# A Mamba and expert layer on one core: the bias as one bf16 matmul, one state's C taken from PSUM, scattering DMAs set to other steps

## The chip, the core and the metric

The kernel runs on one core of a Trainium2 chip. The core has five engines with an in-order queue each: TensorE (PE), VectorE (DVE), ScalarE (ACT), GpSimd (POOL) and SyncE (SP, which here only issues DMAs). The metric is the device time of one execution in microseconds. Three runs of the kernel before gave 952.07, 952.93 and 959.26 us; the median is 952.93.

## The reference, cut to what matters

The input x is 8 sequences of 512 tokens with 128 features. Two branches work on the normalized x: a Mamba layer that runs forward and backward over the sequence, and a router that sends each token to one of 8 experts. Both are added to x.

```python
def mamba(x, ...):                                # f: forward, b: on x[:, ::-1]
    xi, z = split(x @ in_w.T)                     # 256 channels each
    xi = silu(causal_conv(xi) + conv_b)
    dt, Bm, Cm = split(xi @ x_w.T, [8, 8 + 16])   # 16 states
    delta = softplus(dt @ dt_w.T + dt_b)
    h[t] = h[t-1] * exp(delta[t] * A) + delta[t] * u[t] * Bm[t]   # for each state
    y[t] = sum over states of h[t] * Cm[t]
    return ((y + xi * Dp) * silu(z)) @ out_w.T
out = concat([out_f, out_b]) @ combine_w.T + combine_b
...
e = argmax(xn @ router_w.T)                       # expert of each token
ffn = (silu(xn @ gate_w[e].T) * (xn @ up_w[e].T)) @ down_w[e].T
```

The change touches three places of it: the addition of `combine_b`, the product `h * C` of one state, and when the tokens are written out in the order of their experts.

## The kernel before, in words

**Units, states, steps.** A unit is one sequence in one direction; there are 16, f and b in turn (unit 0 is f, 1 is b, 2 is f and so on). A unit has 16 states, and one loop step does one state of one unit: step s is state s mod 16 of unit s div 16, 256 steps in all (L1113 to L1136). Channels lie on the partitions in two halves h, tokens along the free dimension.

**One state.** ACT makes `dA = exp(delta * A)` (L771). The term `b` is made in PSUM: either ACT scales the token-major `dut` by B (L787) and PE transposes it back (L800), or PE spreads B's row over the partitions by a bf16 matmul with a selecting weight (L805) and DVE multiplies by `du` (L812). DVE scans `h` over the tokens (L818, twice 128x512). POOL multiplies `hs` by C for both halves at once (`times_c`, L841, 128x1024). C's row, spread over 128 partitions, comes from DRAM as the tile `cs`: SP issues that DMA three steps ahead (L778), into one of 6 buffers. PE then adds the state into `py` by transposes (L855, `sum_up`, three steps later). In the last unit only, for states 11, 13 and 15, C is spread by a PE matmul into PSUM (`spread_c`, L830), no `cs` is loaded, and DVE does the product as two 128x512 instructions (L839). That choice is `c_in_psum`. The PSUM tile comes from the pool `ps_mm` (2 banks), which nearly everything else that PE makes uses too.

**Around the states.** A plan, written out by hand as (step, kind), calls other work between the states. `prepare(v)` makes unit v's inputs during unit v-1: at its step 9 `log1p` on POOL (L689, and L691 where DVE does not add the last term), at 9 also `split(1)`, at 11 and 12 `delta` on DVE (L698 and the following lines), which reads what `log1p` made (`w`) and what PE made (`pd`, L650). `conclude(v)` finishes unit v during unit v+1: the gate on DVE, two turns by PE, at step 7 and 8 `project` (L914, four token blocks in two halves, into the PSUM tile `po`), at step 9 `total`, where DVE adds `po` to `xt` (L929). In an f unit `project` ends each half with a float32 matmul of one row of ones with `combine_b` (L921, 1x256). In b units there is no bias.

**Scattering.** When the experts of all tokens are known, 32 indirect DMAs write the tokens in the order of the experts (`scatter`, L409). POOL issues them, one at the start of a step ("ev"), at step `35 + i*37//32`, so from 35 to 70 without the steps 42, 49, 57 and 64. Step 35 to 47 is unit 2, 48 to 63 is unit 3 (49 and 57 are free there), 64 to 70 unit 4. At step 73 SP loads the first group of sorted tokens (L434), which waits for all scatters. Within a step, what `prepare` put at "ev" stands ahead of the scatter, and both stand ahead of the step's product on POOL.

**Setup.** POOL fills the constants (L129 to L175), then weights (L185), then `selector` (L194); `split` follows when ACT has made `cdt` (L646). All weights come in one packed tensor `pk`; `combine_b` is its row 0.

Of the kernel before, what the change touches and what calls it, by code (L numbers as in the profile page):

```python
# [33 lines left out]
BF16 = mybir.dt.bfloat16  # L34
# [5 lines left out]
P = 128  # L40
EPS = 1e-5
DIRS = ("f", "b")
L, D, DI, R, NS, KC, E = 512, 128, 256, 8, 16, 4, 8
NH, NJ = DI // P, L // P
# [5 lines left out]
LAST_BY_ACT, LAST_C = BY_ACT + (4, 6, 10, 12, 14), (11, 13, 15)  # L50

ROWS, ROW_C, ROW_DT = 3 * NS, 64, 96
NX = ROW_DT + R


def columns():
# [20 lines left out]
def block_kernel(ctx: ExitStack, tc: tile.TileContext, a: dict, out: bass.AP):  # L77
    nc = tc.nc
    x = a["x"]
    NB = x.shape[0]  # L80
    NT = NB * NJ
# [8 lines left out]
    const, big, tmp = pool("const", 1), pool("big", 1), pool("tmp", 1)  # L90
    two, stp, rep, ffn = pool("two", 2), pool("stp", 4), pool("rep", 6), pool("ffn", 4)
# [12 lines left out]
    at, width = columns()  # L104
    pk = const.tile([P, width], F32, name="pk")
# [10 lines left out]

    rout = pk[:, at["rout"]]
    comb = halves("comb", D)
    comb_b = pk[0:1, at["comb_b"]]
    w = {}  # L120
    for i, d in enumerate(DIRS):
        w[d, "in"] = pk[:, at[d, "in"]]
# [29 lines left out]
    ones = const.tile([P, P], F32, name="ones")  # L152
# [35 lines left out]
    def selector():  # L188


        nothing = const.tile([P, 1], F32, name="nothing")
        nc.vector.memset(nothing, 0.0)
        for k in range(3):
            nc.gpsimd.affine_select(  # L194
                out=sel,
                in_=sel if k else nothing[:ROWS].unsqueeze(2).to_broadcast([ROWS, NS, P]), compare_op=ALU.not_equal, fill=1.0,
                base=-k * NS, pattern=[[-1, NS], [0, P]], channel_multiplier=1,
            )

    def project_weights(d, di):  # L200
        mo = const.tile([P, NH, D], F32, name=f"{d}_mo")
# [206 lines left out]
    def scatter(t):  # L408
        i = nc.gpsimd.indirect_dma_start(  # L409
            sorted_in[:, :], bass.IndirectOffsetOnAxis(ap=M["row"][:, t : t + 1], axis=0),  # L410
            xn[t // 8][:, t % 8, :], None,
        )

        tc.declare_no_dep(i.ins, group="scatter", reason="every token has a row of its own")
        tc.add_to_no_dep_group("scatter", i.ins)
# [106 lines left out]
    units = [(b, d) for b in range(NB) for d in DIRS]  # L522
# [236 lines left out]
        return s % NS in sets.get(s // NS, BY_ACT)  # L759

    def c_in_psum(s):
        return s >= NSTEP - NS and s % NS in LAST_C

    def decay(s):

# [107 lines left out]
    def conclude(v):  # L873
        b, d = units[v]
        c = C[v]

        def gate(ks=range(0, NJ, 2)):
            if "yt" not in c:
                c["yt"] = tmp.tile([P, NJ, DI], F32, tag="yt", name=f"yt_{v}")
            for k in ks:  # L880
                nc.vector.tensor_mul(
                    c["yt"][:, k : k + 2], c["py"][:, k : k + 2], c["z"][:, k : k + 2]
                )

        def turned(dst, j, h):
            if d == "f":
                nc.tensor.transpose(dst, c["yt"][:, j, h * P : (h + 1) * P], ident)
            else:
                nc.tensor.matmul(
                    dst, c["yt"][:, NJ - 1 - j, h * P : (h + 1) * P], exch,  # L890
                    start=True, stop=True,
                )

        def block(y, h, j):
            return y[:, h, j, :] if len(y.shape) == 4 else y[:, h, j * P : (j + 1) * P]

        def back(h):

            p = c["pyb", h] = mm([P, L], f"pyb_{v}{h}")
            for j in range(NJ):  # L900
                turned(p[:, j * P : (j + 1) * P], j, h)

        def back_end(h):
            if h == 0:
                c["y"] = tmp.tile([P, NH, L], F32, tag="y", name=f"y_{v}")
            nc.scalar.copy(c["y"][:, h, :], c["pyb", h])

        def project(js=range(NJ), whole=True):
            if whole or js[0] == 0:
                c["po"] = mm([P, NJ, D], f"po_{v}_{js[0]}")  # L910
            p = c["po"]
            for j in js:
                for h in range(NH):
                    nc.tensor.matmul(  # L914
                        p[:, j, :], block(c["y"], h, j), w[d, "mo"][:, h, :],
                        start=(h == 0 and (d == "b" or j == js[0])),
                        stop=(d == "b" and h == NH - 1), skip_group_check=(d == "f"),
                    )
            if d == "f":

                nc.tensor.matmul(  # L921
                    p[:, js[0] : js[-1] + 1, :], ones[0:1, :],
                    comb_b.unsqueeze(1).to_broadcast([1, len(js), D]),
                    start=False, stop=True, skip_group_check=True,
                )

        def total(js=range(NJ)):
            xs = xt[:, b * NJ + js[0] : b * NJ + js[-1] + 1, :]
            nc.vector.tensor_add(xs, c["po"][:, js[0] : js[-1] + 1], xs)  # L929

        def by_pairs():

            y = tmp.tile([P, NJ, NH, P], F32, tag="y", name=f"y_{v}")
            c["y"] = y.rearrange("p j h t -> p h j t")
            pairs = [range(k, k + 2) for k in range(0, NJ, 2)]
            for i, js in enumerate(pairs):
                gate((NJ - 2 - js[0],) if d == "b" else (js[0],))
                p = c["pyb", i] = mm([P, 2, NH, P], f"pyb_{v}{i}")
                for j in js:
                    for h in range(NH):  # L940
                        turned(p[:, j - js[0], h, :], j, h)
                copy = nc.scalar.copy if i == 0 else nc.vector.tensor_copy
                copy(y[:, js[0] : js[-1] + 1], p)
            for js in pairs:
                project(js)
                total(js)
                nc.sync.dma_start(
                    out[b].rearrange("(j p) h -> p j h", p=P)[:, js[0] : js[-1] + 1, :],
                    xt[:, b * NJ + js[0] : b * NJ + js[-1] + 1, :],
                )  # L950

        if v == len(units) - 1:
            return [(2, "dv", by_pairs)]
        do = lambda f, *k: lambda: f(*k)
        return [
            (2, "dv", gate),
            (3, "pe2", do(back, 0)), (4, "ev", do(back_end, 0)),
            (4, "pe2", do(back, 1)), (5, "ev", do(back_end, 1)),
            (7, "pe", do(project, range(2), False)),
            (8, "pe", do(project, range(2, NJ), False)), (9, "dv", total),  # L960
        ]

# [8 lines left out]
    def add(step, kind, f):  # L971
        plan[step, kind].append(f)
# [29 lines left out]
    for i, kind in (  # L1002
        (0, "dv"), (1, "ev"), (1, "dv"), (1, "pe2"), (2, "ev2"), (2, "dv"),
        (3, "dv"), (4, "ev"), (4, "dv"), (5, "ev"),
    ):
        add(o + i, kind, lambda: next(order_of, None))
    for i in range(NT):
        add(o + 6 + i * 37 // NT, "ev", lambda i=i: scatter(i))

    begin = 4  # L1010
    groups = [list(range(k, min(k + GROUP, NK))) for k in range(0, NK, GROUP)]
# [37 lines left out]
        pass  # L1049
    weights("f")  # L1050
    selector()
    first.norm()
    first.turn()
    first.turn_end()
# [155 lines left out]
```

## Time and profile before

| | busy us | share of the span | instructions |
|---|---|---|---|
| PE matmul | 850.2 | 89% | 5510 |
| PE weight load | 657.9 | 69% | 5510 |
| DVE | 907.2 | 95% | 1101 |
| ACT | 803.0 | 84% | 1490 |
| POOL | 841.5 | 88% | 524 |

The profiled execution has a span of 951.6 us and a time of its own of 953.34 us. The granted PE clock was 0.953 on average. Where the kernel's lines spend their time:

| line | what | count | busy us | mean ns |
|---|---|---|---|---|
| L841 | POOL product with C, 128x1024 | 253 | 594.3 | 2362 |
| L818 | DVE scan, 128x512 | 512 | 592.8 | 1206 |
| L839 | DVE product with C from PSUM, 128x512 | 6 | 3.8 | 679 |
| L830 | PE matmul that spreads C | 6 | 3.4 | 640 |
| L914 | PE projection, f units | 128 | 16.9 | 275 |
| L921 | PE bias, 1x256 float32 | 32 | 11.1 | 425 |
| L805 | PE spreading B, 48x512 bf16 | 125 | 50.6 | 405 |
| L409 | POOL issues a scatter | 32 | 32.5 | 1015 |
| L689 | POOL part of log1p, 128x1024 | 15 | 35.4 | 2361 |

A float32 matmul appears as two instructions, and matmuls overlap, so their means are longer than the time from one start to the next. "Idle before" of an instruction is how long its engine stood still ahead of it, with the engine and line that ended the wait.

### The profile page before, as it was taken

How to read it: one execution, taken by the hardware profiler on the slowest of the kernel's cores; microseconds unless marked ns; L12 is line 12 of the kernel's file. 1: busy time of each engine (PE TensorE's matmuls, PEld its weight loads, DVE VectorE, ACT ScalarE, POOL GpSimd, SP SyncE). 2: the span in 40 equal slices, each digit the busy share in tenths (PEclk: the TensorE clock that was granted, in tenths of full speed). 3: DMA queues.
4: the chain of work that ended last, by engine and by line, in shares of the span. 5: the costliest groups of instructions: out<-in, count | busy, mean ns of one | idle time of the engine just before them, and what ended most of it. 6: DMA issues, size and time to landing. Idle time of an engine off the chain costs nothing.

```text
span 951.6 us, 16224 instructions
## 1 busy us (share of the span) xinstructions
PE 850.2 (89%) x5510; PEld 657.9 (69%) x5510; DVE 907.2 (95%) x1101; ACT 803.0 (84%) x1490; POOL 841.5 (88%) x524
## 2 busy tenths in 40 slices
PE   5699896978789889899998999989999999989897
PEld 2367574766567668777786877868777786767676
DVE  7999989999899999999999999999999999999996
ACT  5898986969679797998969989698988979799792
POOL 5689798799999979799897998979899898979995
PEclk9588999988979999999899999999999999999999
DMA  5364222222233625245441544425245341622262
GB/s 153 111 132 107 66 76 66 78 74 80 84 95 104 192 70 182 78 123 163 114 154 53 161 138 121 152 82 185 63 130 168 112 153 54 186 74 85 90 177 75
DMA packets 68483, 108.54 MB, mean 114 GB/s; under 512 B 6848, under 2 KB 29248, under 8 KB 68400
## 3 DMA queue, kind: packets, MB, share of 16 engines
q1 hardware_dynamic: 65552, 101.32, 36.0%
q0 software_dynamic: 2272, 4.67, 1.4%
q10 hardware_dynamic: 576, 1.51, 0.5%
q8 instruction: 44, 0.72, 0.3%
q14 instruction: 39, 0.32, 0.1%
HBM read 97.60 MB, written 9.87 MB: 113 GB/s over the span
## 4 chain that ended last, share of the span: by engine, by line
PE 42%; ACT 26%; DVE 18%; issue 7%; POOL 6%; DMA 1%; SPq 0%; POOLq 0%; DVEq 0%; ACTq 0%
PE py L855 14%; DVE hs L818 10%; ACT dA L771 8%; PE b L800 7%; ACT dbt L787 7%; PE pg L457 4%; PE pd L650 4%; POOL hs L841 3%; DVE b L812 3%; DVE acc L590 2%; PE pde L489 2%; PE po L914 2%; PE b L805 2%; ACT acc L582 1%; PE pdu L714 1%
## 5 line engine op out<-in xcount | busy, mean ns | idle before, releaser
L841 POOL TENSOR_TENSOR hs<-hs,cs 128x1024 f32<-128x1024 f32 x253 | 594.3, 2362 | 71.9 <-DVE hs L818 59.9
L818 DVE TENSOR_TENSOR_SCAN hs<-dA,b 128x512 f32<-128x512 f32 x512 | 592.8, 1206 | 0.1
L855 PE MATMUL py<-ident,hs 128*128 128x128 f32 x2048 | 279.3, 282 | 10.8 <-POOL hs L841 10.7
L855 PEld LDWEIGHTS py<-ident,hs 128*128 128x128 f32 x2048 | 234.4, 145 | 47.2 <-POOL hs L841 23.6
L787 ACT ACTIVATE dbt<-dut,bt 128x256 f32<-128x256 f32 x524 | 221.9, 496 | 0.1
L800 PE MATMUL b<-ident,dbt 128*128 128x128 f32 x1048 | 187.5, 289 | 19.6 <-DVE hs L818 10.4
L771 ACT ACTIVATE dA<-delta,b_A 128x512 f32<-128x512 f32 x256 | 168.2, 715 | 14.9 <-DVE hs L818 14.8
L800 PEld LDWEIGHTS b<-ident,dbt 128*128 128x128 f32 x1048 | 128.8, 145 | 74.1 <-ACT dbt L787 52.7
L771 ACT ACTIVATE dA<-delta,f_A 128x512 f32<-128x512 f32 x256 | 168.6, 715 | 8.3 <-DVE hs L818 6.3
L812 DVE TENSOR_TENSOR b<-du,b 128x512 f32<-128x512 f32 x250 | 159.8, 686 | 9.3 <-PE b L805 8.5
L599 PE MATMUL pz<-pk,xin 128*128 128x256 f32 x128 | 42.8, 492 | 29.3 <-DVE acc L590 25.4
L650 PE MATMUL pd<-cdt,pk 9*128 9x512 f32 x124 | 66.3, 635 | 0.0
L590 DVE SCALAR_TENSOR_TENSOR acc<-pi,pk,acc 128x511 f32<-128x511 f32 (+2 forms) x96 | 64.5, 739 | 0.1
L457 PE MATMUL pg<-xeT,we 128*128 128x128 f32 x468 | 61.8, 278 | 2.2 <-ACT z L610 2.1
L457 PEld LDWEIGHTS pg<-xeT,we 128*128 128x128 f32 x468 | 56.2, 192 | 5.5 <-ACT z L610 3.8
L599 PEld LDWEIGHTS pz<-pk,xin 128*128 128x128 f32 x128 | 30.2, 247 | 41.1 <-ACT dbt L787 26.5
L805 PE MATMUL b<-cdt,sel 48*128 48x512 bf16 x125 | 50.6, 405 | 8.6 <-DVE hs L818 8.6
L721 ACT COPY dut<-pdu 128x512 f32<-128x512 f32 x32 | 18.6, 585 | 34.6 <-PE pdu L714 34.6
L500 POOL DMA_INDIRECT by_token<-ye,to x39 | 39.6, 1016 | 6.3 <-issue 3.1
L646 POOL TENSOR_TENSOR cdt<-cdt 32x512 f32<-32x512 f32 (+1 forms) x32 | 33.1, 1034 | 7.8 <-ACT cdt L632 7.7
L489 PEld LDWEIGHTS pde<-we,g 128*128 128x128 f32 x234 | 27.6, 191 | 15.2 <-issue 7.6
L409 POOL DMA_INDIRECT sorted_in<-xn,row_i x32 | 32.5, 1015 | 5.3 <-issue 3.8
(170 smaller groups left out, 1054.8 us busy)
## 6 DMA issues: line engine op xcount, KB each, us to landing
cs<-cd SPq DMA_DIRECT2D x253, 256.0 KB, 3.5
we<-in_expert_w SPq DMA_DIRECT2D x39, 576.0 KB, 4.6
sorted_in<-empty SPq DMA_DIRECT2D x9, 258.0 KB, 7.9
xe<-sorted_in SPq DMA_DIRECT2D x9, 258.0 KB, 4.5
xt<-in_x SPq DMA_DIRECT2D x8, 256.0 KB, 7.3
moe<-by_token SPq DMA_DIRECT2D x8, 256.0 KB, 3.0
out<-xt SPq DMA_DIRECT2D x7, 256.0 KB, 3.7
pk<-in_pack ACTq DMA_DIRECT2D x1, 704.0 KB, 7.9
```

Source lines behind the costliest of these rows:

```text
L457: nc.tensor.matmul(p[:, q - 4 * b, :], T[ks[i]][:, which, c, :], G[ks[0], "xT"][:, i, :], start=True, stop=True,)
L590: nc.vector.scalar_tensor_tensor(c["acc"][:, h, k:], c["pi", h][:, : L - k], cw[:, h, KC - 1 - k : KC - k], c["acc"][:, h, k:], ALU.mult, ...
L599: nc.tensor.matmul(p[:, j, :], c["xin"][:, t : t + P], w[d, "in"][:, DI:], start=True, stop=True,)
L650: nc.tensor.matmul(p, w[d, "dt"][:, h * P : (h + 1) * P], cdt[ROW_DT : NX + 1], start=True, stop=True,)
L771: nc.scalar.activation(k["dA"][:, h, :], c["delta"][:, h, :], AF.Exp, scale=w[d, "A"][:, h, n : n + 1],)
L787: nc.scalar.activation(k["dbt"][:, j, :], c["dut"][:, j, :], AF.Copy, scale=c["bt"][:, j, n : n + 1],)
L800: nc.tensor.transpose(k["b", h][:, j * P : (j + 1) * P], k["dbt"][:, j, h * P : (h + 1) * P], ident,)
L805: nc.tensor.matmul(k["b", 0], sel[:, n, :], c["bc"], start=True, stop=True)
L812: nc.vector.tensor_mul(k["b", h], c["du"][:, h, :], k["b", 0])
L818: nc.vector.tensor_tensor_scan(k["hs"][:, h, :], k["dA"][:, h, :], k["b", h], 0.0, ALU.mult, ALU.add)
L841: nc.gpsimd.tensor_mul(k["hs"], k["hs"], k["cs"].unsqueeze(1).to_broadcast([P, NH, L]))
L855: nc.tensor.matmul(c["py"][:, j, h * P : (h + 1) * P], block[:, h, j * P : (j + 1) * P], weight, skip_group_check=True, **kw,)
```

## The change

It has three parts. The bias: `combine_b` is packed three times, on rows 0 to 2; at the start POOL takes from rows 0 and 1 what bf16 keeps of them, and from row 0 once more, so that the upper halves of the three rows are three bf16 pieces of the float32 bias. `project` of an f unit then begins with one bf16 matmul of 3 rows and 512 columns over the whole of `po`, instead of ending each half with a float32 one. The product: in unit 3, state 6 (step 54), C goes the way of the last unit's states 11, 13, 15. The scatters: 32 steps from 35 to 71, without 40, 48, 52, 55 and 66.

```diff
+SCATTER, SCATTER_C = 3, (6,)
...
-    comb_b = pk[0:1, at["comb_b"]]
+    comb_b = pk[0:3, at["comb_b"]]
+    bias = comb_b.bitcast(BF16).rearrange("p (n two) -> p n two", two=2)[:, :, 1]
+    one_row = const.tile([3, P], BF16, name="one_row")
+    nc.gpsimd.memset(one_row, 1.0)
...
+    def bias_pieces():
+        for m in (2, 1):
+            nc.gpsimd.tensor_sub(comb_b[:m], comb_b[:m], bias[:m])
...
     def c_in_psum(s):
-        return s >= NSTEP - NS and s % NS in LAST_C
+        return s % NS in {SCATTER: SCATTER_C, len(units) - 1: LAST_C}.get(s // NS, ())
...
         def project(js=range(NJ), whole=True):
-            if whole or js[0] == 0:
+            new = whole or js[0] == 0
+            if new:
                 c["po"] = mm([P, NJ, D], f"po_{v}_{js[0]}")
             p = c["po"]
+            if new and d == "f":
+                nc.tensor.matmul(
+                    p, one_row, bias.unsqueeze(1).to_broadcast([3, NJ, D]),
+                    start=True, stop=False, skip_group_check=True,
+                )
             for j in js:
                 for h in range(NH):
                     nc.tensor.matmul(
                         p[:, j, :], block(c["y"], h, j), w[d, "mo"][:, h, :],
-                        start=(h == 0 and (d == "b" or j == js[0])),
-                        stop=(d == "b" and h == NH - 1), skip_group_check=(d == "f"),
+                        start=(d == "b" and h == 0), stop=(h == NH - 1),
+                        skip_group_check=(d == "f"),
                     )
-            if d == "f":
-                nc.tensor.matmul(
-                    p[:, js[0] : js[-1] + 1, :], ones[0:1, :],
-                    comb_b.unsqueeze(1).to_broadcast([1, len(js), D]),
-                    start=False, stop=True, skip_group_check=True,
-                )
...
+    dates = [s for s in range(o + 6, o + 6 + 37) if s not in (40, 48, 52, 55, 66)]
     for i in range(NT):
-        add(o + 6 + i * 37 // NT, "ev", lambda i=i: scatter(i))
+        add(dates[i], "ev", lambda i=i: scatter(i))
...
     selector()
+    bias_pieces()
...
-    pack[0, at["comb_b"]] = inputs[pre + "combine_b"]
+    pack[:3, at["comb_b"]] = inputs[pre + "combine_b"]
```

(`o` is 29 there, so that `o + 6` is step 35.)

## The prediction

> **What bounds the kernel.** First the busy table: DVE is busy 95% of the span, so its idle time is what can be won. DVE's timeline lists each idle stretch with what ended it. Between step 0 and the last 50 us these are mostly 0.2 to 1 us of waiting for PE, and two larger waits for POOL, with a third, small one behind them:
>
> ```profile
> 196.97 0.70 DVE L698 SCALAR_TENSOR_TENSOR pd<-pd,w 128x512 f32<-128x512 f32 x1 [1.85 <-POOL w L691]
> ...
> 257.56 0.70 DVE L698 SCALAR_TENSOR_TENSOR pd<-pd,w 128x512 f32<-128x512 f32 x1 [4.02 <-POOL w L689]
> ...
> 313.96 0.70 DVE L698 SCALAR_TENSOR_TENSOR pd<-pd,w 128x512 f32<-128x512 f32 x1 [0.18 <-POOL w L689]
> ```
>
> The bracket is DVE's idle time before `delta`. All three are where `delta` needs POOL's `log1p`, called at steps 41, 57 and 73, for units 3, 4 and 5. Next POOL's timeline there:
>
> ```profile
> 251.84 1.01 POOL L409 DMA_INDIRECT sorted_in<-xn,row_i  x1 [0.17 <-issue]
> 252.88 2.34 POOL L841 TENSOR_TENSOR hs<-hs,cs 128x1024 f32<-128x1024 f32 x1
> 255.18 2.35 POOL L689 TENSOR_TENSOR w<-q,w 128x1024 f32<-128x1024 f32 x1
> ...
> 306.90 4.71 POOL L841 TENSOR_TENSOR hs<-hs,cs 128x1024 f32<-128x1024 f32 x2
> 311.56 2.37 POOL L689 TENSOR_TENSOR w<-q,w 128x1024 f32<-128x1024 f32 x1
> ```
>
> From 170.97 to 329 us POOL's only idle time is the 0.17 before each scatter. A product with its scatter takes about 3.57 us there, about a DVE step. POOL is behind: at 252.88 it starts the product of step 56, while DVE has ended the scans of step 59 at 253.54. So from 171 to 314 `log1p` arrives when POOL's list is done, and the list sets the time. After 329 POOL waits again (5.35 us at 346 for a scan), and DVE leads, with PE close behind. The f units' bias is in PE's timeline, here of unit 9, where unit 8 is projected, with DVE beside it:
>
> ```profile
> 588.30 0.40 PE L805 MATMUL b<-cdt,sel 48*128 48x512 bf16 x1
> 588.63 1.09 PE L855 MATMUL py<-ident,hs 128*128 128x128 f32 x8
> ...
> 590.77 0.69 PE L921 MATMUL po<-pk,ones 1*128 1x256 f32 x2
> 591.39 1.16 PE L457 MATMUL pg<-xeT,we 128*128 128x128 f32 x8
> ```
> ```profile
> 592.59 0.69 DVE L481 TENSOR_TENSOR g<-g,pg 128x512 f32<-128x512 f32 x1 [0.38 <-PE pg L457]
> ...
> 602.64 0.69 DVE L698 SCALAR_TENSOR_TENSOR delta<-pd,w 128x512 f32<-128x512 f32 x1 [0.24 <-PE pd L650]
> ```
>
> PE runs without a gap there, and DVE twice waits for it behind the bias.
>
> **Scatters and the product.** A scatter costs POOL 1.01 + 0.17 = 1.18 us, wherever it stands; all 32 stay. A product costs 2.33 from start to start (4.66 for two: 2.36 + 2.30). Before step 41's `log1p` stand 6 scatters now and 5 then: the 1.85 wait falls by 1.18. Step 42 takes one instead, so POOL is level again. Before step 57's stand 20 now and 18 then, and the product of step 54 is gone: 2 x 1.18 + 2.33 = 4.69, so `w` ends at 257.53 - 4.69 = 252.84. DVE takes over that product as two instructions, 1.28 us a pair at the end of this kernel, 1.20 to the next start. It comes to `delta` at 253.54 - 1.18 - 0.35 (a wait for `po` at 247.20, below) + 1.20 = 253.2. So the 4.02 wait goes and 4.3 us are won there.
>
> Then it is partly handed back. Before step 73's `log1p` stand 32 scatters in both kernels, so POOL's list is shorter by the product alone: `w` ends at 313.93 - 2.33 = 311.60. DVE, which came at 313.78, comes at 309.5 and waits 2.1. What remains is 313.96 - 311.62 = **2.34 us**. POOL cannot run out of work meanwhile: its smallest lag behind DVE's scan in the stretch is 3.4 us (step 67, scan end 289.49, product 292.89), and there POOL is earlier by 2.33 + 1.18, one product and one scatter, and DVE by 4.3: the lag grows.
>
> Beside that, at no cost: PE's C matmul (1.05 us in the chain of the last unit) lies where PE waits for POOL (14 us of waits for POOL's products from 206 to 262); were that cover gone it would cost its 1.05. It takes one of the two banks of `ps_mm`, and PE's `pd` now stands behind DVE's product; `pd` began at 238.28, and the scan before the product ended at 236.29, so bank and PE are ready in time, and a delay up to 4 us would fall into the wait that goes. One `cs` DMA less. The last scatter goes from step 70 to 71, and SP's load of sorted tokens waits for it (3.4 us now); `cs` loads queue behind that. It is POOL's list that sets when it is issued: 303.54 now, about 303.4 then. The `cs` load issued behind it at 306.98 lands 3.5 later and is used at 321.82: 11 us of room. At the start POOL makes the pieces: two instructions smaller than the 1.03 of L646, within its 7.68 us of waiting before 22.08; the memset, bounded by the 0.20 of a larger one, before constants that PE needs only at 8.8.
>
> **The bias.** In the chain of waits two such bias pairs take 0.62 and 0.63, and L805, the nearest row to the new matmul (512 bf16 columns), takes 0.33. So PE does 0.62 + 0.63 - 0.33 = 0.92 us less in each f unit. By the Trainium skill (TensorE: Matmul & The Clock Gate, "Wait — 56ns, not 53.3ns?") 512 columns follow each other at 215.7 ns at full clock; by that it would be 1.03. The trace's 0.33 has a weight load with it, as the new one has. What of the 0.92 reaches DVE is bounded by zero and by DVE's waits for PE right behind it: for unit 4's projection 0.17, for unit 6's 0.35 + 0.40 + 0.24, capped at 0.92, for 8, 10 and 12 0.62, 0.61, 0.62; 2.94 in sum. Unit 0's waits (0.35, 0.33, 1.06, at most 0.92) lie before DVE's waits for the router through ACT and POOL (0.51, 0.65), unit 2's in POOL's stretch, unit 14's (1.75) in the last 50 us, whose chain is POOL's (`hs` L841 21%, `xt` L519 10%): I take nothing for these, and 0.92 each for units 0 and 14 as a bound. PE's lead can be lost at the next wait of PE for DVE or ACT; some 13 us later DVE waits 0.46 for PE anyway (616.51). I take half of 2.94, **1.5 us**, between 0 and 4.8.
>
> Sum: 2.34 + 1.5 = 3.8. The profiled span of 951.6 becomes 947.8, its time of 953.34 becomes 949.5. That run stands 0.41 over the median of 952.93, so the median becomes **949.1 us**.
>
> **Rivals.**
> - PE's lead is kept whole: 2.34 + 2.9 to 4.8, 945.8 to 947.7. For it: PE has no gap in that stretch. Against it: it waits for ACT and DVE elsewhere. 0.15.
> - PE's lead is lost whole, POOL's gain alone: 950.6. 0.17.
> - The second wait does not come (step 73), because scatters hide in POOL's waits: 4.3 + 1.5, 947.1. Against it: POOL has none there. 0.05.
> - Neither part reaches the end, each gain met by the next wait: 952.9. For it: every DVE wait here is under a microsecond but two. 0.10.
> - Slower, by the granted clock. The windows show it after each lull of PE:
>
> ```profile
> 255.00:260.00 5.00, 2.80 (x16) 1.90 (x17) 2.37 (x4) 0.25 (x1) 5.00 (x4) 1.00 0.19 52
> 260.00:265.00 5.00, 3.02 (x15) 2.30 (x14) 4.93 (x6) 4.13 (x10) 4.64 (x4) 0.68 0.23 67
> 265.00:270.00 5.00, 4.72 (x25) 4.35 (x26) 5.00 (x7) 1.79 (x4) 4.79 (x4) 0.63 0.36 107
> ```
>   The first number after the window's length is PE's busy time, the one behind POOL's is the clock. A kernel in which PE starts at other times, with less to do, can put such stretches where DVE waits for PE. Unit 7 shows the price: the granted clock was 0.57 from 470 to 474, with PE busy throughout the 4 us before, and DVE waits 0.48 + 0.39 + 0.35 + 0.40 between 472 and 480, and 0.38 in unit 9 at the same steps: 1.24 more. From four further stretches on the gain is gone: five give 949.1 + 6.2 = 955.3. Against it: the lull at 250 to 260 goes, and no PE gap is added. By the Trainium skill (same page, "What's actually happening") the array falls to half clock after an idle window of about 3.4 us, in windows that run free of the kernel; the trace agrees with 0.63 and 0.68 behind a stretch in which PE was busy 2.80 of 5. 0.06.
>
> **The numbers.** Forecast, 948 to 950.2: 0.47. The range of 946.0 to 953.0 takes in the forecast and the cases of the bias lost, the second wait gone, nothing gained, and most of PE's lead kept; the slow clock and the lowest end are left out. One per cent, 9.5 us, is about what a measurement can tell from no change; every case lies within it, unless many clock stretches move: faster 0.02, same 0.95, slower 0.03.
>
> **What would show it.** Right: no POOL wait of DVE near 253, one of about 2 us near 310, the one at 197 down to 0.7; PE's bias 0.33 once per f unit; no DVE wait behind `po` in units 7, 9, 11, 13. Wrong: POOL idle between 171 and 310, a wait for C at step 54, for `pd` near 239, or `cs` landing late after SP's load of tokens; a changed row of the clock where DVE waits longer for PE.

## The result, and the profile after

The changed kernel was timed three times beside the kernel before, on one chip each time:

| set | before, median us | after, median us | ratio, 95% interval |
|---|---|---|---|
| first | 952.90 | 950.56 | 0.9972, 0.9959 to 0.9986 |
| second | 953.30 | 947.41 | 0.9936, 0.9915 to 0.9956 |
| third | 954.54 | 949.73 | 0.9951, 0.9929 to 0.9973 |

It is faster by 0.3 to 0.6%, which is within the 1% called "same". One execution of all those compared in this document, 1084.7 us at a clock of 0.72 by the kernel with PE filled, is in a slower state and left out. The forecast of 949.1 lies among the three medians, though the first alone, 950.56, is that of the rival with PE's lead lost (950.6). The first two intervals just fail to overlap, and that is a finding of its own (last section).

The profiled execution of the first set has a span of 951.5 us, nearly that of before (951.6). To see why, lay the two traces side by side by steps: the time from the first scan of one step to that of another, read off DVE's timeline. A column shows where a kernel gains, whatever happened earlier. The last column is 16 steps, one unit's length, with unit 10's projection in it, mostly at full clock (57.38 has a half-clock stretch in it).

| kernel (profiled execution) | steps 0-40 | 40-84 | 84-128 | 128-255 | 180-196 |
|---|---|---|---|---|---|
| before | 148.86 | 163.78 | 153.65 | 438.88 | 56.72 |
| after, first set | 147.16 | 161.44 | 157.32 | 439.17 | 56.63 |
| after, second set | 146.36 | 161.42 | 151.56 | 438.55 | 56.65 |
| after, third set | 152.49 | 161.55 | 151.64 | 439.29 | 57.38 |

Steps 40 to 84 hold nearly all of the scattering stretch. There the three executions of the changed kernel agree: 2.34, 2.36 and 2.23 us less than before. In the other columns the same program differs from itself by up to 6 us.

DVE's timeline of the changed kernel (first set; start, length, engine and line, operation, in brackets the idle time ahead and what ended it). L710 is the old L698, L701 the old L689, L842 the old L830:

```profile
193.98 0.70 DVE L710 SCALAR_TENSOR_TENSOR pd<-pd,w 128x512 f32<-128x512 f32 x1 [0.47 <-POOL w L703]
...
221.04 1.29 DVE L893 TENSOR_TENSOR yt<-py,z 128x512 f32<-128x512 f32 x2 [0.72 <-PE py L867]
...
234.63 1.29 DVE L851 TENSOR_TENSOR hs<-hs,c 128x512 f32<-128x512 f32 x2 [1.01 <-PE c L842]
...
309.88 0.70 DVE L710 SCALAR_TENSOR_TENSOR pd<-pd,w 128x512 f32<-128x512 f32 x1 [1.40 <-POOL w L701]
```

The wait of 4.02 us is gone, the first one is down from 1.85 to 0.47, and a new one stands at 309.88. Another is new at 234.63: step 54's C arrives 1.01 late. POOL's timeline ahead of step 73's `log1p` (L853 is the product, formerly L841) is as full as before:

```profile
302.87 4.67 POOL L853 TENSOR_TENSOR hs<-hs,cs 128x1024 f32<-128x1024 f32 x2
307.49 2.35 POOL L701 TENSOR_TENSOR w<-q,w 128x1024 f32<-128x1024 f32 x1
```

`w` starts at 307.49 instead of 311.56, and from 171 to 314 no idle time of POOL is above the 0.17 of a scatter. Of these 4.07 us, 1.74 were won before step 40. So count from the scan of step 40. POOL's last wait of more than 0.2 ends 11.05 ahead of that scan in both kernels, and `w` starts 129.54 behind it before and 127.21 now: 2.33 less, one product. PE's timeline at unit 8's projection has one bias matmul in the place of two pairs of 0.69:

```profile
586.15 0.40 PE L927 MATMUL po<-pk,one_row 3*128 3x512 bf16 x1
586.48 1.16 PE L933 MATMUL po<-f_mo,y 128*128 128x128 f32 x8
```

From its start to the next it takes 0.33. Of the 4.0 us that this execution won by step 84 it lost 3.7 again before step 128. The windows of the same trace show how (after the length: PE, weight loads, DVE, ACT, POOL busy, then the granted clock):

```profile
400.00:405.00 5.00, 5.00 (x34) 3.85 (x34) 5.00 (x7) 5.00 (x11) 4.62 (x5) 1.00 0.04 13
405.00:410.00 5.00, 5.00 (x26) 2.77 (x24) 5.00 (x6) 4.86 (x11) 5.00 (x3) 0.87 0.76 233
410.00:415.00 5.00, 5.00 (x24) 4.66 (x24) 3.69 (x4) 4.88 (x8) 5.00 (x3) 0.50 0.66 197
...
470.00:475.00 5.00, 5.00 (x19) 3.34 (x18) 2.39 (x3) 5.00 (x11) 5.00 (x3) 0.50 0.70 230
```

At a clock of 0.50 DVE is busy 3.69 and 2.39 of 5 us. It waits there 1.30, 0.66, 1.15, 1.69, 0.72 us for PE. In the second set the clock is 1.00 between 405 and 420, and steps 84 to 128 take 5.8 us less.

### The profile page after: what moved, and what is told of

Read it like the earlier page. It is cut to its first block, busy times and chain, and to the rows that moved or that the text cites. A ratio compares the mean times of both kernels' runs of the same rounds, so it can differ in the third digit from the quotient of the medians.

```text
span 951.5 us, 16179 instructions
## 1 busy us (share of the span) xinstructions
PE 851.3 (89%) x5488; PEld 660.0 (69%) x5488; DVE 907.6 (95%) x1103; ACT 804.2 (85%) x1490; POOL 840.5 (88%) x526
## 4 chain that ended last, share of the span: by engine, by line
PE 44%; ACT 22%; DVE 19%; issue 6%; POOL 6%; DMA 1%; SPq 0%; POOLq 0%; DVEq 0%; ACTq 0%
PE py L867 15%; DVE hs L830 10%; ACT dA L783 7%; PE b L812 7%; ACT dbt L799 6%; PE pd L662 5%; PE pg L469 4%; POOL hs L853 4%; DVE b L824 3%; PE pde L501 3%; PE po L933 2%; DVE acc L602 2%; PE b L817 2%; ACT acc L594 1%; PE pdu L726 1%
## 5 line engine op out<-in xcount | busy, mean ns | idle before, releaser
L853 POOL TENSOR_TENSOR hs<-hs,cs 128x1024 f32<-128x1024 f32 x252 | 592.3, 2363 | 73.8 <-DVE hs L830 59.4
L830 DVE TENSOR_TENSOR_SCAN hs<-dA,b 128x512 f32<-128x512 f32 x512 | 592.5, 1204 | 0.1
L867 PEld LDWEIGHTS py<-ident,hs 128*128 128x128 f32 x2048 | 237.0, 146 | 48.6 <-POOL hs L853 25.6
L812 PE MATMUL b<-ident,dbt 128*128 128x128 f32 x1048 | 187.2, 291 | 20.5 <-DVE hs L830 9.7
L812 PEld LDWEIGHTS b<-ident,dbt 128*128 128x128 f32 x1048 | 129.5, 146 | 73.6 <-ACT dbt L799 47.8
```

The costliest lines, as they stand in the source:

```text
L812: nc.tensor.transpose(k["b", h][:, j * P : (j + 1) * P], k["dbt"][:, j, h * P : (h + 1) * P], ident,)
L830: nc.vector.tensor_tensor_scan(k["hs"][:, h, :], k["dA"][:, h, :], k["b", h], 0.0, ALU.mult, ALU.add)
L853: nc.gpsimd.tensor_mul(k["hs"], k["hs"], k["cs"].unsqueeze(1).to_broadcast([P, NH, L]))
L867: nc.tensor.matmul(c["py"][:, j, h * P : (h + 1) * P], block[:, h, j * P : (j + 1) * P], weight, skip_group_check=True, **kw,)
```

## The experiments

**The theory.** POOL's list sets the time of the scattering stretch, and one product less on it gives about 2.3 us; the bias saves PE 0.92 us in each f unit, part of which reaches DVE. **Rivals:** only one of the two parts matters; or the measured gain is a difference of granted clock. Step times of all profiled executions:

| kernel | ratio, 95% interval | 0-40 | 40-84 | 84-128 | 128-255 | 180-196 |
|---|---|---|---|---|---|---|
| bias alone | 0.9973, 0.9945-1.0001 | 149.79 | 163.75 | 152.59 | 438.94 | 56.63 |
| steps of the scatters alone | 0.9985, 0.9965-1.0004 | 151.97 | 164.22 | 152.63 | 438.58 | 56.72 |
| product alone (step 56) | 1.0016, 0.9995-1.0038 | 147.92 | 168.43 | 157.76 | 438.97 | 56.73 |
| product and steps, old bias | 0.9967, 0.9944-0.9991 | 146.98 | 162.02 | 153.63 | 438.69 | 56.73 |
| second product | 0.9950, 0.9932-0.9968 | 149.90 | 163.08 | 151.58 | 438.50 | 56.66 |
| PE filled | 0.9978, 0.9960-0.9996 | 146.39 | 161.50 | 151.98 | 438.84 | 56.67 |
| no bias | 0.9962, 0.9947-0.9977 | 148.72 | 162.20 | 151.92 | 438.66 | 56.60 |
| steps 46, 47 free | 0.9935, 0.9913-0.9958 | 146.60 | 162.12 | 151.67 | 439.07 | 56.66 |
| both | 0.9973, 0.9953-0.9993 | 146.43 | 161.78 | 151.67 | 439.35 | 57.38 |
| four bias matmuls | 0.9973, 0.9946-1.0000 | 148.74 | 161.60 | 151.96 | 440.62 | 56.65 |

All ratios are to the kernel before, timed in the same set. The first four kernels are one set, the next three belong to the second set of the changed kernel, the last three to the third. The diffs of the steps alone, the product alone, and product and steps are against the kernel before, all others against the changed kernel; they are cut to the lines that matter.

### The bias alone

```diff
-        return s % NS in {SCATTER: SCATTER_C, len(units) - 1: LAST_C}.get(s // NS, ())
+        return s >= NSTEP - NS and s % NS in LAST_C
...
-        add(dates[i], "ev", lambda i=i: scatter(i))
+        add(o + 6 + i * 37 // NT, "ev", lambda i=i: scatter(i))
```

> Only the bias is changed: one bf16 matmul of three pieces, C of step 54 from DRAM and the scatters at their old steps. Theory (POOL's list gives 2.3 us, PE's bias about 1.5): 0 to 2.9 us less than before, likeliest 1.5, and all three POOL waits of DVE as before (1.85 near 197, 4.02 near 253, about 0.2 near 314). Rival A, PE's 0.92 us per f unit never reaches DVE: 0.0. Rival B, the bias gives all of the measured 2.7 and POOL's part nothing: 2.7 less here, and 0 for the kernel without the bias's change. The bias shows once per f unit at 0.33, in the place of two pairs of 0.62.

The stretch is unchanged (163.75 against 163.78). But the wait near 253 was not "as before". DVE's timeline of this kernel:

```profile
245.19 1.22 DVE L690 SCALAR_TENSOR_TENSOR w<-q,one 128x1024 f32<-128x1024 f32 x1 [3.52 <-PE one L697]
...
258.19 0.70 DVE L710 SCALAR_TENSOR_TENSOR pd<-pd,w 128x512 f32<-128x512 f32 x1 [2.09 <-POOL w L701]
```

PE waited 1.37 at 237 for POOL's product, its `pd` (four matmuls) took 3.78 where it takes 1.98 at full clock, and DVE stood 3.52 behind it. The later wait for POOL shrank in exchange. Time lost inside the stretch costs nothing as long as POOL's list ends last. The ratio alone does not tell 1.5 us from nothing, and by it rival B (2.7) fits as well. Of the 2.7 between the means, 1.1 go with the clock (0.952 on average against 0.950, at 4.6 us for each 0.01 in this set's runs of before). The 16 steps from 180 do tell: 56.63 against 56.72, 0.09 us for one projection, where half of DVE's waits of 0.61 behind unit 10's was expected.

### The steps of the scatters alone

```diff
+    dates = [s for s in range(o + 6, o + 6 + 37) if s not in (40, 48, 52, 55, 66)]
     for i in range(NT):
-        add(o + 6 + i * 37 // NT, "ev", lambda i=i: scatter(i))
+        add(dates[i], "ev", lambda i=i: scatter(i))
```

> Only the steps of the scatters are changed. Theory: all 32 scatters stand ahead of step 73's log1p in both kernels, so nothing is won at the end: 0.0 us. On the way DVE's wait near 197 falls from 1.85 to about 0.7, the one near 253 from 4.02 to about 2.8 (list shorter by 2 x 1.18, DVE earlier by 1.18), and the one near 314 grows from 0.2 to about 2.5, which hands the 2.4 back. Rival: the gaps themselves win, because scatters later fall into time that POOL has free: 2.4 us less.

DVE's timeline of this kernel:

```profile
198.47 0.70 DVE L698 SCALAR_TENSOR_TENSOR pd<-pd,w 128x512 f32<-128x512 f32 x1 [0.40 <-POOL w L691]
...
257.80 0.70 DVE L698 SCALAR_TENSOR_TENSOR pd<-pd,w 128x512 f32<-128x512 f32 x1 [2.29 <-POOL w L689]
...
316.64 0.70 DVE L698 SCALAR_TENSOR_TENSOR pd<-pd,w 128x512 f32<-128x512 f32 x1 [1.90 <-POOL w L689]
```

The handing back, by itself: 0.40, 2.29 and 1.90 instead of 1.85, 4.02 and 0.18. Waiting moves from the first two to the third, and the stretch takes 164.22, no less than before. The new steps alone give nothing there.

### The product alone, in step 56

```diff
+SCATTER, SCATTER_C = 3, (8,)
...
-        return s >= NSTEP - NS and s % NS in LAST_C
+        return s % NS in {SCATTER: SCATTER_C, len(units) - 1: LAST_C}.get(s // NS, ())
```

> Only the product is changed, and with the scatters at their old steps it is that of step 56 that goes to DVE in place of step 54's (step 57, which follows, has no scatter). Theory: POOL's list is shorter by one product from then on, so 2.3 us less than before with no new date at all; DVE's wait near 253 falls from 4.02 to about 0.5 to 1.7 (list 2.33 shorter, DVE 1.2 later), the one near 314 stays small. Rival A, DVE pays 1.2 us for the product and a wait for C of about 1.0 on PE, and both count: 0 to 0.2 less. Rival B, the new dates are needed: 0.

The theory's 2.3 us less did not come, and rival A was too mild: the stretch takes 4.65 us more. DVE's timeline, then PE's:

```profile
245.10 1.29 DVE L840 TENSOR_TENSOR hs<-hs,c 128x512 f32<-128x512 f32 x2 [5.07 <-PE c L831]
...
254.51 0.69 DVE L930 TENSOR_TENSOR xt<-po,xt 128x512 f32<-128x512 f32 x1 [2.02 <-PE po L922]
```
```profile
235.41 1.09 PE L856 MATMUL py<-ident,hs 128*128 128x128 f32 x8 [1.35 <-POOL hs L842]
236.44 3.78 PE L651 MATMUL pd<-cdt,pk 9*128 9x512 f32 x4
...
243.94 1.12 PE L831 MATMUL c<-cdt,ident 16*128 16x512 f32 x2
```

C of step 56 is the last thing in PE's step 55, behind `pd` and behind a `py` that waits for the late POOL. The clock there is 0.64 to 0.68, and `pd` takes 3.78 instead of 1.98, so part of the wait is the clock's. C came at 245 and DVE had stood since 240. POOL, with its shorter list, then waits for DVE twice, 1.56 and 1.90 us, and its `w` of step 73 starts later than in the kernel before (130.59 behind the scan of step 40 against 129.54). In step 54 C stands ahead of `pd`, and arrives 1 us late. So the place of the product can cost more than the product wins: it takes work off POOL but puts DVE behind PE, and PE is behind POOL. The scatters stand at their old steps here, and step 54 was not tried with these, so how much is the place, the scatters' steps or the clock is not shown.

### Product and steps, with the old bias

```diff
+SCATTER, SCATTER_C = 3, (6,)
...
-        return s >= NSTEP - NS and s % NS in LAST_C
+        return s % NS in {SCATTER: SCATTER_C, len(units) - 1: LAST_C}.get(s // NS, ())
...
+    dates = [s for s in range(o + 6, o + 6 + 37) if s not in (40, 48, 52, 55, 66)]
     for i in range(NT):
-        add(o + 6 + i * 37 // NT, "ev", lambda i=i: scatter(i))
+        add(dates[i], "ev", lambda i=i: scatter(i))
```

> Step 54's product on DVE and the new steps of the scatters, with the old float32 bias. Theory: 2.3 us less than before (2.0 to 2.7), the wait near 253 gone, one of 1.4 to 2.1 near 310. With the bias alone it should add up to the whole change's 2.7 to 3.8. Rival, the bias alone is worth it: 0. Rival, the measured gain is a difference of granted clock: the gain follows the mean granted clock of the runs, about 3 us for each 0.01, and not the parts.

The ratio, 0.9967, is as good as that of the whole change in the first set; the stretch takes 162.02, 1.8 less than before. The wait of 1.4 to 2.1 expected near 310 did not come. POOL's `w` of step 73 is as early as in the changed kernel (127.42 behind the scan of step 40), but DVE comes later still: it waits 1.61 for `py` near 221 and 0.97 for `b` at 245, the latter behind 10 us with the clock at 0.65 to 0.67. The bias is not what wins there. Behind unit 8's projection DVE's timeline of this kernel has the two waits of before:

```profile
588.41 0.69 DVE L482 TENSOR_TENSOR g<-g,pg 128x512 f32<-128x512 f32 x1 [0.39 <-PE pg L458]
...
598.46 0.69 DVE L699 SCALAR_TENSOR_TENSOR delta<-pd,w 128x512 f32<-128x512 f32 x1 [0.24 <-PE pd L651]
```

In the changed kernel (second set) both are gone, and one stands further on. DVE's timeline, PE's and POOL's:

```profile
602.88 1.29 DVE L824 TENSOR_TENSOR b<-du,b 128x512 f32<-128x512 f32 x2 [0.88 <-PE b L817]
```
```profile
600.91 0.66 PE L726 MATMUL pdu<-ident,du 128*128 128x128 f32 x4 [0.49 <-POOL du L721]
...
602.39 0.40 PE L817 MATMUL b<-cdt,sel 48*128 48x512 bf16 x1
```
```profile
597.27 2.36 POOL L853 TENSOR_TENSOR hs<-hs,cs 128x1024 f32<-128x1024 f32 x1
599.59 1.26 POOL L721 TENSOR_TENSOR du<-delta,u 128x512 f32<-128x512 f32 x1
```

PE comes earlier by what the bias saved and then waits 0.49 for POOL's `du`, which stands behind a product; the kernel before has no such gap of PE there. DVE gets `b` no sooner and waits 0.88. That is where the bias's gain ends: 56.65 us for the 16 steps from 180, against 56.72 and 56.73 with the old bias.

This `du` in the kernel before, in POOL's timeline:

```profile
606.92 1.27 POOL L709 TENSOR_TENSOR du<-delta,u 128x512 f32<-128x512 f32 x1
```

It starts 34.02 behind the scan of step 148 (572.89) before and 34.05 behind it (565.54) in the changed kernel, and 34.0 to 34.1 in all 14 profiled executions, with the bias old, new, absent or four times as long. From 0.33 behind that scan to 44.7 behind it POOL has no wait above the 0.17 of an issue. So POOL's list sets the time here too. DVE does get nearly all of PE's 0.92: it is 0.91 ahead of the kernel before just ahead of this `b`, and 0.08 ahead after it. The steps show it in every profiled kernel but that with four matmuls: 152 to 156 take 15.30 or 15.31 with the old bias and 14.78 or 14.79 with the new or none, 156 to 160 then 12.56 or 12.57 against 12.99 to 13.04.

### The changed kernel again

> The changed kernel as it is, beside the same runs of before as the three that follow. If the parts add, it lies near the sum of the bias alone (ratio 0.9973 measured) and of product and steps alone (0.9967), so at 0.994, or 5 to 6 us less; if they share one slack, at 0.9972 again, 2.7 us less. Its mean granted clock says how much of either is clock: about 3 us for each 0.01 in the 20 runs so far.

The ratio is that of the sum, 0.9936. But the step times say that it is not the parts that add: the stretch is 2.36 as in the first set, and 4.6 of the 7.3 us between the two spans (944.3 and 951.6) lie in steps 0 to 40 and 84 to 128.

> The changed kernel once more, as the reference on the same chip for the three that follow. The two ratios so far are 0.9972 [0.9959, 0.9986] and 0.9936 [0.9915, 0.9956], which do not overlap. If the half-clock stretches make that difference, this one has a ratio between the two and its time goes with the stretches of its profile where DVE waits for PE; the parts alone (0.9973 and 0.9967) add up to 0.994.

A ratio in between, and a profiled span of 951.3: here steps 0 to 40 take 3.6 us more than before and the stretch again 2.23 less. The clock in that first part was 0.83 (last section).

### A second product, in step 70

```diff
-        return s % NS in {SCATTER: SCATTER_C, len(units) - 1: LAST_C}.get(s // NS, ())
+        return s % NS in {SCATTER: SCATTER_C, 4: (6,), len(units) - 1: LAST_C}.get(s // NS, ())
...
-    dates = [s for s in range(o + 6, o + 6 + 37) if s not in (40, 48, 52, 55, 66)]
+    dates = [s for s in range(o + 6, o + 6 + 37) if s not in (40, 48, 52, 55, 71)]
```

> The changed kernel with one more state's C from PSUM, step 70 in unit 4, and step 71 instead of 66 free of a scatter. Theory (POOL's list is what step 73's log1p waits for, and PE's C of that step is ready): the wait of 1.40 near 310 is gone, the product costs DVE 1.20, so 0 to 0.2 less than the changed kernel. Rival A, C comes late as at step 56 in the experiment with the product alone (5.07 there): 1 to 4 us more. Rival B, POOL's list goes on setting the time after step 73: 2.3 less.

The wait near 310 is gone, and DVE waits for C twice:

```profile
238.37 1.29 DVE L851 TENSOR_TENSOR hs<-hs,c 128x512 f32<-128x512 f32 x2 [1.38 <-PE c L842]
...
296.39 1.28 DVE L851 TENSOR_TENSOR hs<-hs,c 128x512 f32<-128x512 f32 x2 [0.60 <-PE c L842]
```

The stretch takes 163.08, 1.7 more than in the changed kernel beside it, so rival A's sign is right. POOL's list did get shorter by a product again (`w` of step 73 starts 124.93 behind the scan of step 40, against 127.19). Now that POOL's list no longer ends last, DVE pays in full for the product (1.20), for the wait for C and for one of 1.58 for `py` at 224. The first product was worth it since those waits lay in time that POOL's list took anyway.

### Steps 46 and 47 free, and both together

```diff
-    dates = [s for s in range(o + 6, o + 6 + 37) if s not in (40, 48, 52, 55, 66)]
+    dates = [s for s in range(o + 6, o + 6 + 37) if s not in (40, 46, 47, 55, 66)]
```

> The changed kernel with the steps 46 and 47 free of a scatter instead of 48 and 52: as many scatters as before ahead of steps 57 and 73, but two fewer instead of one ahead of the products that unit 2's py waits for. Theory (POOL's list reaches DVE through PE too: DVE's wait of 0.7 to 1.6 for py near 221 and of 0.8 to 1.4 for C near 234 come from PE's sum_up waiting for POOL's product): both waits fall together by 1.0 to 1.2, and are handed back at step 73, whose list is as long as before (wait 1.40 to about 2.5): 0 against the changed kernel. Rival, these two waits are PE's own work and do not move, so 0 too, but with both waits as before. Second rival, the gain is kept: 1 us less.

The first half came as the theory says: the waits for `py` near 221 and for C near 234 are gone from the timeline, which shows those above 0.15. So POOL's lag does reach DVE through PE. They were not handed back at step 73 alone, whose wait is 1.19 and not 2.5; DVE also waits 0.40 for `py` at 278 and 0.86 at 297. In DVE's timeline:

```profile
297.02 1.22 DVE L690 SCALAR_TENSOR_TENSOR w<-q,one 128x1024 f32<-128x1024 f32 x1 [0.86 <-PE one L697]
309.10 0.70 DVE L710 SCALAR_TENSOR_TENSOR pd<-pd,w 128x512 f32<-128x512 f32 x1 [1.19 <-POOL w L701]
```

The stretch takes 162.12, 0.6 more than in the changed kernel beside it. The ratio of 0.9935, the best of all, does not come from the stretch, and its interval overlaps that of the changed kernel beside it (0.9951): not shown to be better.

The second kernel also has the second product, with 71 free instead of 66.

> The free steps 46 and 47, and the second product (step 70) with step 71 free: the list ahead of step 73 is one product shorter, so that nothing is handed back there. Theory: 1.0 to 1.2 won near 221 to 234, 1.4 near 310, less 1.2 for the product and 0.6 for its wait for C: 0.6 to 0.8 less than the changed kernel, too little to be seen alone in the times but seen in DVE's waits between 170 and 330 (4.1 in the changed kernel, 2.0 or less here). Rival (the second product alone came out 2 us above the changed kernel on the same chip): 1 to 2 more.

DVE's listed waits between 170 and 330 sum to 3.3, where 2.0 or less was expected and the changed kernel has 4.1; with 1.2 of product on DVE nothing is left (161.78). The ratio is the rival's, 2 us above the changed kernel, though the intervals overlap.

### No bias, and four bias matmuls

The first of these two kernels leaves `combine_b` out of the result.

```diff
-            if new and d == "f":
+            if False:
...
-                        start=(d == "b" and h == 0), stop=(h == NH - 1),
+                        start=(h == 0 and (d == "b" or j == 0)), stop=(h == NH - 1),
```

> The changed kernel without any matmul for the bias: combine_b is left out of the result. It bounds what the bias on PE can still be worth: PE does 0.33 us less in each of 8 f units. Theory (PE's time behind po reaches DVE at half to full rate): 0.5 to 2.0 us less than the changed kernel. Rival, PE's lead is lost at its next wait and only waits of DVE right behind po counted: 0 to 0.3 less.

```diff
                     start=True, stop=False, skip_group_check=True,
                 )
+                for _ in range(3):
+                    nc.tensor.matmul(
+                        p, no_row, bias.unsqueeze(1).to_broadcast([3, NJ, D]),
+                        start=False, stop=False, skip_group_check=True,
+                    )
```

> The changed kernel with three more matmuls of zero weights behind the bias's, 0.99 us of PE in each f unit, a little more than what the change took from PE there (0.92); the result is unchanged. Theory (PE's time behind po is what the bias's change gives): 1.5 to 2 us more than the changed kernel, which undoes the bias's part. Rival A, PE has slack there and the bias alone won its 2.6 by granted clock: 0 to 0.3 more. Rival B, every microsecond of PE there counts in full: 5 to 8 more. It shows once per f unit as four matmuls of 0.33 each.

Steps 180 to 196 take 56.60 with no bias, 56.63 to 56.65 with one matmul, 56.65 with four, and 56.72 or 56.73 with the old form. The bias on PE goes from nothing to 1.25 us (0.62 + 0.63) and DVE's time changes by 0.13. The four, in PE's timeline:

```profile
583.82 0.40 PE L929 MATMUL po<-pk,one_row 3*128 3x512 bf16 x1
584.06 0.86 PE L934 MATMUL po<-pk,no_row 3*128 3x512 bf16 x3
584.85 1.16 PE L940 MATMUL po<-f_mo,y 128*128 128x128 f32 x8
```

They take 1.03 together, about 0.26 each, not 0.33. The kernel with four has a ratio 0.0022 above the changed kernel's, as the theory wanted, but the trace puts its 1.3 to 2.1 us of steps 128 to 255 elsewhere. In steps 148 to 164 it takes 58.08 instead of 56.64, and this is the clock there (half from 580.2 to 583.6, before the four begin):

```profile
580.00:585.00 5.00, 5.00 (x23) 3.71 (x24) 4.46 (x5) 4.88 (x8) 5.00 (x3) 0.66 0.68 181
```

The kernel with no bias has the higher ratio (0.9962 against 0.9936, intervals overlapping a little), which no theory has: differences of 0.002 in a ratio settle nothing here.

### PE filled in its lull

```diff
+FILL = 8
...
+    zeros = const.tile([ROWS, P], BF16, name="zeros")
+    nc.gpsimd.memset(zeros, 0.0)
...
+    def fill(s):
+        if s >= NSTEP or by_act(s):
+            return
+        _, n, c, k = part(s)
+        for _ in range(FILL):
+            nc.tensor.matmul(
+                k["b", 0], zeros, c["bc"], start=False, stop=True, skip_group_check=True
+            )
...
+            if s % NS == 2:
+                fill(s + 2)
```

> The changed kernel, with PE kept busy while DVE makes the convolution's sum in each unit: 8 matmuls of zero weights that add nothing, added to the b of the state after next, at step 2 of each unit, ahead of pz, where PE now waits 1.89 for DVE's acc. Theory that lulls of PE set off the stretches of half clock, and that these cost the run-to-run spread: the mean granted clock rises from 0.951 to 0.96 or more, fewer half-clock stretches after 330 us, and by about 3 us for each 0.01 some 2 to 3 us less than the changed kernel. Rival A, the stretches come however PE is filled there: clock 0.951, and 0 to 3 us more by the added matmuls (8 x 0.22 to 0.33 a unit, behind which b and pz stand). Rival B, the clock rises but costs nothing: same time at a higher clock.

The mean granted clock rose, to 0.966 over the executions compared, from 0.951 for the changed kernel in its three sets and 0.956 in the set beside it. After 330 us two half-clock stretches of 3.4 us are left, where the three profiled executions of the changed kernel have 20.5, 23.9 and 47.8 us of them. The lull of 1.89 ahead of `pz` is now filled and the one of 1.01 stays, in PE's timeline at one such place:

```profile
616.05 1.97 PE L828 MATMUL b<-cdt,zeros 48*128 48x512 bf16 x8
...
621.07 0.63 PE L815 MATMUL b<-ident,dbt 128*128 128x128 f32 x4 [1.01 <-DVE hs L843]
```

The ratio is 0.9978, above the changed kernel's 0.9936 in that set. So this lull has a part in the half-clock stretches, and the fill removes most of them, but the time does not follow: rival B, perhaps with some of A's price. In the profiled execution the clock between 640 and 900 us is 1.00, and steps 128 to 255 take 438.84, against 438.55 for the changed kernel with its stretches.

## Why the prediction was right, and where it was not

- **One product less on POOL's list, 2.34 us: right**, in its path and its size. Three executions give 2.34, 2.36 and 2.23. The wait near 253 is gone and the one near 197 is 0.47 to 0.61 (0.7 predicted). The list itself shows it in every profiled kernel but that with step 56's product: `w` of step 73 starts 129.5 behind the scan of step 40 in the three that keep POOL's list whole (before, bias alone, steps alone), 127.2 to 127.4 in the eight without step 54's product, 124.9 and 125.0 in the two with another taken off. The stretch gains that much only where DVE is there in time: with the product and the old bias it is 1.8, without a bias 1.6. The handing back is shown by the steps alone, which give nothing.
- **"It comes at 309.5 and waits 2.1": mis-sized.** 1.40, 1.39 and 0.74 were measured. Two waits ahead of it, for `py` and for C, hold DVE back. The end does not move, as it is POOL's.
- **PE's C matmul at no cost: right in the sum, wrong in its reason.** "Bank and PE are ready in time" failed: DVE waited 1.01, 0.81 and 0.48 for C, which the prediction itself lists as a sign of being wrong. Its "14 us of waits for POOL's products" as cover adds the waits of PE's weight loads (9.4) to those of its matmuls (5.0), which overlap: PE as a whole had 5.0 us of them. The wait for C falls "into the wait that goes", as the prediction said of any delay up to 4 us. In step 56, and with a second product, the same wait counted.
- **The bias, 1.5 us: the step that failed.** PE's 0.92 is right (0.33 in the place of 0.62 and 0.63). "Half of 2.94" is not. Around unit 8's, 10's and 12's projections 0.09, 0.09 and about 0.0 us were won, where half of 0.62 was taken. "PE's lead can be lost at the next wait": nearly all of it reaches DVE, and is then lost at PE's wait for POOL's `du`. The waits of 0.38 and 0.24 became one of 0.88. The reading that failed is "After 329 POOL waits again [...] and DVE leads": POOL waits there, but for 44 us of each of these units its list is full, and it is the list that `du`, PE's next matmuls and DVE's `b` wait for. For unit 6's projection the traces give 0.1 as well (steps 120 to 128, where no half clock is: 27.87 with the old bias, 27.77 to 27.84 with the new or none), for unit 4's at most 0.4 (steps 88 to 96: 27.29 before, 26.90 in the changed kernel).
- **The rivals.** By the traces the mechanism is that of "PE's lead is lost whole" (950.6, given 0.17). What the profiled executions show beyond it lies in the columns 0-40 and 84-128: the kernel before loses 1.6 us in steps 120 to 124 at half clock (16.87, where two experiments with the old bias take 15.30), which the changed kernel's second and third execution do not; the first loses more than that there. That the medians lie on both sides of 949.1 is therefore luck as far as these traces show: they account for 2.5 to 3.0 us and not for 3.8. Slower by the granted clock did not come, but its price did, in the first profiled execution (3.7 us more than before in steps 84 to 128).
- **Open:** 2.3 us from POOL's list, and 0.2 to 0.7 from the bias, are shown in the step times. The ratios stand for 2.7, 6.1 and 4.7. The mean clock does not explain the rest: in the third set it is 0.949 for the changed kernel and 0.950 for the kernel before, and the changed kernel is 4.5 us faster in the mean. Whether the rest is half-clock stretches at other places, or a gain that these traces don't show, was not settled: the bias alone, which wins 0.1 in 16 steps, has a ratio of 0.9973 as well, with an interval that reaches 1.

## What to carry to other kernels

When an engine's list sets the time of a stretch, count what stands on the list ahead of the last thing that is waited for: moving items within it only moves the wait, and taking one off is worth its full length until the next engine's waits take over; a second one here was worth less than nothing. A gain on an engine that runs without a gap holds only as far as that engine's next wait, so look for what feeds it there (here POOL's full list, twice) before counting any of it; an engine that waits now and then can still set the time of the stretch between two of its waits. And where executions of one program differ by more than the change is worth, compare step times stretch by stretch in several traces; the total does not say which part won.

## What the runs showed of the hardware

The same program's time goes with the clock that it is granted. Over 89 executions of the kernel before, beside the experiments, the mean clock went from 0.941 to 0.958 and the time from 950.7 to 962.3 us, with 4.0 us for each 0.01 (correlation -0.80). Part of it is decided early. The windows from 33 to 180 us for two executions of the changed kernel, of the third and of the second set:

```profile
33.00:180.00 147.00, 130.12 (x714) 98.14 (x714) 136.81 (x170) 124.85 (x241) 119.82 (x86) 0.83 0.28 79
```
```profile
33.00:180.00 147.00, 129.72 (x750) 95.05 (x750) 142.29 (x176) 130.16 (x253) 125.23 (x90) 0.90 0.32 86
```

PE is busy as long in both, at a clock of 0.83 and 0.90, with 714 and 750 matmuls done. Steps 0 to 40 take 152.49 and 146.36 us. Among all profiled kernels the four slowest there (149.8 to 152.5) have 0.83 to 0.88 in this row and the five fastest (146.4 to 147.0) 0.90 to 0.93, though the kernel before has 0.90 as well and takes 148.86.

But the mean does not set the time. With the lull filled the clock was higher by 0.010 than in the changed kernel beside it, which at that slope would be 4 us, and nothing was won. By the step times, what counts is whether DVE waits for PE when the clock is halved: the changed kernel's second execution has four such stretches in steps 128 to 255, which take it 438.55, and the filled kernel one, in 438.84.

Nor was a long lull needed. By the Trainium skill (TensorE: Matmul & The Clock Gate, "What's actually happening") the array falls to half clock after an idle window of about 3.4 us. In the first profiled execution of the changed kernel PE's longest waits in the 20 us ahead of the stretch that begins near 409 are 1.89, 1.01 and 0.49, between 390 and 398, and PE has no gap from then on. The clock is 1.00 in the window from 400 to 405 and 0.50 in that from 410 to 415. No longer lull preceded the fall here, and it came some 10 us behind these. In the kernel before, the stretch that the prediction shows begins at 261.8, and PE's longest wait in the 15 us ahead of it is 2.82, so its "the trace agrees" is too strong for the length of the window. By the same section of the Trainium skill the windows run free of the kernel. The traces agree: within each of the 14 profiled executions all changes of the clock lie on a grid of 3.41 us, half-clock stretches last one to five of its steps (but for the last, which the program's end cuts), and where the grid lies against the program's start differs between executions.
